# Layer 1 of a convolution and Mamba kernel: the norm's squares one step earlier, root and Newton behind the decay of scan 18, B's transposes behind a sum of y

## The chip, the core and the metric

The kernel runs on one core of a Trainium2 chip, as one launch. The metric is device time in microseconds (us), the median of several runs. A profile comes from one execution of its own, and its times are from the start of its span.

The engines of the core: PE (TensorE, matrix multiply; PEld is its weight load), DVE (VectorE), ACT (ScalarE, activation functions and copies), POOL (GpSimd) and SP (SyncE, which here only issues DMA transfers). Each engine runs its own queue of instructions in order and waits for others by semaphores. PE writes its results to PSUM, a small memory of eight banks; SBUF is the larger working memory.

## The reference

The input is 32 images of 96 channels and 56 x 56 pixels, in float32. Layer 0 is an inverted bottleneck convolution. Layer 1, in which the change lies, takes each image as a sequence of 3136 tokens with 96 channels and passes it through two Mamba blocks, then a fusion with a global branch and a batch norm. One block:

```
mu = seq.mean(-1); var = ((seq - mu) ** 2).mean(-1)
h = (seq - mu) * rsqrt(var + 1e-5) * ln_g + ln_b
xs, z = split(h @ in_w)                       # 192 channels each
xc = silu(causal_conv4(xs) + conv_b)
dt, Bm, Cm = split(xc @ xproj_w)              # 6, 16 and 16 columns
delta = softplus(dt @ dt_w + dt_b)
h_t = exp(delta * A) * h_(t-1) + delta * Bm * xc      # 192 channels x 16 states
y = (sum over states of h_t * Cm + Dp * xc) * silu(z)
seq = seq + y @ out_w
```

## The kernel before

**Units and steps.** In layer 1 each sequence is cut into four chunks of 784 tokens. A unit is one chunk in one of the two blocks, so there are 32 x 4 x 2 = 256 units, block 1 following block 0 at some distance. A unit holds 24 scans: three channel blocks k of 64 channels, in each four groups j of four states, and two halves p of the channels. Each scan is one instruction on DVE (line 1052) over 128 partitions (32 channels x 4 states) and 784 tokens, 1.84 us long.

**An order written out by hand.** The loop at the end of layer 1 goes through steps, one scan each. In a step it calls the work around that scan in a fixed sequence: inject (POOL: the product u x B for the two scans four steps on, line 1041), steps of the lists with small fractions, seed (ACT: D x xc into the PSUM bank of y, line 1086), decay (ACT: exp(delta x A) for the next scan, line 1004), bring (ACT: a copy cp of C into PSUM, line 1029), the bursts (Silu and Softplus with their table loads, lines 677 and 678), the scan, gated (DVE: y times the gate z, line 1110), product (DVE: state times C for the first 416 tokens, line 1060), save (ACT: last states, line 1077), rest (POOL: state times C for the other tokens, line 1068), fill (PE: the product u x B for the scans with j = 0, that is scans 0, 1, 8, 9, 16 and 17 of a unit, line 1018, into PSUM, tile bp), then listed steps with fractions from 0.05 to 0.08, reduce (PE: the sum over states into y, line 1099), and the listed steps with larger fractions. For scans with j = 0 the decay goes to SBUF (tile bx) and is computed two or three steps ahead. The PSUM tiles da and bp share two buffers, so each scan's decay or fill has to wait until the scan two before it is done.

**Listed steps.** prepare(n) returns the work that gets unit n ready as pairs (time, function). The time is counted in scans from the start of unit n - 2; the whole part names the step, the fraction the place in it. A time of -10.98 thus lies in step -11 with fraction 0.02. Modulo 24, the steps from -12 to -4 are scans 12 to 20 of an earlier unit, in which the work of the next units also runs. The steps that matter here:

- center(h), line 702: PE subtracts the channel mean from half h of the chunk (tile cen, PSUM).
- square(h), line 707: ACT squares it (tile sx, SBUF).
- variance, line 712: PE sums the squares with seven one-column matmuls, each of which is two instructions (tile var, PSUM). The fourth needs squares of both halves.
- root, lines 719 to 721: ACT adds epsilon (tile va), takes Ln and then Exp with scale -0.5, so that rs is about 1/sqrt(var). Line 723 copies the tail of the chunk before into xn.
- newton, lines 729, 731 and 734: three DVE operations refine rs.
- turn (line 744, PE, tile ct), normalise (line 751, ACT, tile sx_t), turn_back (line 757, PE, tile xn in PSUM), normal (line 761, ACT): the normalised chunk, channel by channel.
- project_bc (line 798, PE, tile bc) and store_bc (line 802, ACT, tile bcs, then two DMA stores): B, C and the input of delta, for the unit that follows.
- turn_b (line 822, PE, tile bt) and diagonal (lines 831 and 832, ACT): B's transposes for the diagonals of the fills; scatter sends them to DRAM eight steps later.
- project_dt (line 810), turn_u and keep_u (lines 848, 854 and 855): delta and the transposed u.

All of cen, var, ct, xn, xs, z, bc, bt, dt, ut and o share two PSUM banks (pool l1p). A new tile in this pool waits until the last reader of the tile that had the bank is done. Here bc takes over the bank of var.

In the step with scan 17, ACT's queue has, after the Silu burst of the step before: va, Ln, Exp, the tail copy, decay of scan 18, cp, a state copy, decay of scan 19, then bcs, four of normalise 0, decay of scan 20, cp, a state copy, the two copies of bt, three of normalise 1, and decay of scan 21.

Of the kernel before, what the change touches and what calls it, by code (L numbers as in the profile page):

```python
# [35 lines left out]
TK = 112  # L36
NK = LC // TK
# [23 lines left out]
def conv_mamba_kernel(ctx, tc, a, out):  # L61
# [43 lines left out]
    with ExitStack() as ph:  # L105
# [119 lines left out]
        for i in range(NHB):  # L225
            t = hp3.tile([128, H + 2, W + 2], F32, name=f"hpad{i}", tag=f"hpad{i}")
# [303 lines left out]
    with ExitStack() as ph:  # L530
# [14 lines left out]
        def bank(name):  # L545
            return pp.tile([128, 512], F32, name=name, tag="p")

        def wt(shape, tag, bufs, n):
            return work.tile(shape, F32, name=f"{tag}_{n}", tag=tag, bufs=bufs)
# [132 lines left out]
        def cols(h):  # L682
            return slice(h * HB, h * HB + HB)

        def prepare(n):
# [7 lines left out]
            d = data[n]  # L693
# [6 lines left out]
            def center(h):  # L700
                ps = d["cen", h] = bank(f"cen_{n}_{h}")
                pe.matmul(ps[:C, :HB], cen, seqs[c, i][:, cols(h)], start=True, stop=True)

            def square(h):
                if h == 0:
                    d["sq"] = wt([128, LC], "sx", 1, n)[:C]
                s.activation(d["sq"][:, cols(h)], d["cen", h][:C, :HB], AF.Square)
# [7 lines left out]
            def root():  # L715

                va = d["va"] = wt([TK, NK], "va", 1, n)
                rs = d["rs"] = d["var"][:TK, 16 : 16 + NK]
                s.activation(va, d["var"][:TK, :NK], AF.Identity, bias=epsc[:TK])
                s.activation(rs, va, AF.Ln)  # L720
                s.activation(rs, rs, AF.Exp, scale=-0.5)
                if q > 0:
                    s.copy(xn[:, : KC - 1], tails[i])

            def newton(step):
                va, rs = d["va"], d["rs"]
                if step == 0:
                    d["nw"] = wt([TK, NK], "nw", 1, n)
                    v.scalar_tensor_tensor(d["nw"], rs, -0.5, va, ALU.mult, ALU.mult)
                if step == 1:  # L730
                    v.tensor_mul(d["nw"], d["nw"], rs)
                if step == 2:
                    to = wt([TK, NK], "rs", 1, n)
                    v.scalar_tensor_tensor(to, d["nw"], 1.5, rs, ALU.add, ALU.mult)  # L734
                    d["rs"] = to
                    if q == 0:
                        g.memset(xn[:, : KC - 1], 0.0)
# [40 lines left out]
            def keep(tag, bufs, ps, k):  # L778
                if k == 0:
                    d[tag] = wt([128, NB, HB], tag, bufs, n)  # L780
                if tag == "dl":
                    s.activation(d[tag][:, k, :], d[ps, k][:, :HB], AF.Identity, bias=dp[:, i, k, 0:1])
                else:
                    s.copy(d[tag][:, k, :], d[ps, k][:, :HB])  # L784

            def gate(k):
                ps = d["zp", k] = bank(f"z_{n}_{k}")
                for h in range(2):
                    pe.matmul(  # L789
                        ps[h * 64 : h * 64 + 64, :HB], wz[:, i, k * 64 : k * 64 + 64],  # L790
                        xn[:, KC - 1 + h * HB : KC - 1 + h * HB + HB], start=True, stop=True,
                    )
# [73 lines left out]

            steps = [(-20.5, load)]
            for h in range(2):
                steps += [((-11.9, -10.94)[h], lambda h=h: center(h)), ((-10.98, -9.99)[h], lambda h=h: square(h))]
            steps += [(-9.94, variance), (-7.9, root), *[(t, lambda m=m: newton(m)) for m, t in enumerate((-6.3, -6.2, -6.1))]]  # L870
            for m in range(2):
                steps += [((-6.7, -5.5)[m], lambda m=m: turn(m)), (-5.7 + m, lambda m=m: normalise(m))]
                steps += [(-4.5 + m, lambda m=m: turn_back(m)), (-3.9 + m, lambda m=m: normal(m))]
# [4 lines left out]
            for k in range(NB):  # L878
                steps += [(t, lambda k=k, o=o: conv(k, o)) for o, t in taps[k]]
                steps += [((3.1, 5.1, 6.1)[k], lambda k=k: keep("xc", 3, "xs", k))]  # L880
                steps += [((11.06, 11.07, 12.06)[k], lambda k=k: gate(k)), ((12.01, 12.02, 13.01)[k], lambda k=k: keep("z", 3, "zp", k))]
            steps += [(17.6, project_bc), (18.2, store_bc), (18.6, turn_b), (19.2, diagonal)]
            for k in range(NB):
                steps += [((20.6, 21.5, 21.6)[k], lambda k=k: project_dt(k)), ((21.2, 22.1, 22.2)[k], lambda k=k: keep("dl", 1, "dtp", k))]
                steps += [((43.5, 53.6, 56.06)[k], lambda k=k: turn_u(k)), ((44.1, 54.2, 57.01)[k], lambda k=k: keep_u(k))]
# [59 lines left out]
        def place(t):  # L945
            k, r = divmod(t, 2 * SG)
            return k, r // 2, r % 2
# [38 lines left out]
        def by_pe(at):  # L986

            return place(at % NT)[1] == PEJ

        def lend(at):  # L990

            if by_pe(at) and at % 2 == 0:
                to = wt([128, 2, LC], "bx", 3, at)
                for p in range(2):
                    das[at + p] = to[:, p, :]

        def decay(at):

            n, t = divmod(at, NT)
            i, d = units[n][1], data[n]  # L1000
            k, j, p = place(t)
            if not by_pe(at):
                das[at] = dpool.tile([128, 2 * 512], F32, name=f"da_{at}", tag="da")[:, :LC]
            s.activation(das[at], d["delta", k][:, p, :], AF.Exp, scale=acol[:, j, i, 2 * k + p : 2 * k + p + 1])  # L1004
# [18 lines left out]
        def bring(at):  # L1023

            n, t = divmod(at, NT)
            k, j, p = place(t)
            if p == 1:
                cps[at] = cpool.tile([128, LP], F32, name=f"cp_{at}", tag="cp")
                s.copy(cps[at], data[n]["C", j][:, :LP])  # L1029
# [5 lines left out]
        def inject(at):  # L1035

            n, t = divmod(at, NT)
            k, j, p = place(t)
            if p == 0 and j != PEJ:
                bx = wt([128, 2, LC], "bx", 3, at)  # L1040
                g.tensor_mul(bx, data[n]["u", k], beside(data[n]["B", j]))  # L1041
                for p in range(2):
                    bxs[at + p] = bx[:, p, :]
# [35 lines left out]
        def seed(at):  # L1079

            n, t = divmod(at, NT)
            k, j, p = place(t)
            if j == 0 and p == 1:
                i, d = units[n][1], data[n]
                yps[k] = ypool.tile([128, 512], F32, name=f"y_{n}_{k}", tag="y")
                s.activation(yps[k][:, :HB], d["xc"][:, k, :], AF.Copy, scale=dp[:, i, k, 1:2])  # L1086
# [17 lines left out]
        def gated(at):  # L1104

            n, t = divmod(at, NT)
            k, j, p = place(t)
            if j == SG - 1 and p == 1:
                d = data[n]
                v.tensor_mul(d["z"][:, k, :], d["z"][:, k, :], yps.pop(k)[:, :HB])  # L1110

        total = len(units) * NT
        todo, early = {}, {}
        for n in range(len(units)):
            steps, bursts = prepare(n)
# [9 lines left out]
        def ahead(at):  # L1125

            return (2, 1) if at % NT == 0 else (3, 2)
# [5 lines left out]
        with tc.manual_schedule():  # L1133
            for at in range(min(todo), max(todo) + 1):
                for m in (2, 3):
                    if 0 <= at + m < total and by_pe(at + m) and (at + m) % 2 == 0 and ahead(at + m)[0] == m:
                        lend(at + m)
                if 0 <= at + 4 < total:
                    inject(at + 4)
                for u, step in todo.get(at, ()):  # L1140
                    if u < 0.05:
                        step()
                if 0 <= at - LAG < total:
                    seed(at - LAG)
                if 0 <= at + 1 < total and not by_pe(at + 1):
                    decay(at + 1)
                for x in range(at, at + 5):
                    pair = x // 2 * 2
                    if 0 <= x < total and by_pe(x) and pair - ahead(pair)[x - pair] == at:
                        decay(x)  # L1150
                if 0 <= at < total:
                    bring(at)
                for step in early.get(at, ()):
                    step()
                if 0 <= at < total:
                    scan(at)
                if 0 <= at - LAG - 1 < total:
                    gated(at - LAG - 1)
                if 0 <= at - 1 < total:
                    product(at - 1)  # L1160
                if 0 <= at - 2 < total:
                    save(at - 2)
                if 0 <= at < total:
                    rest(at)
                if 0 <= at + 1 < total and by_pe(at + 1):
                    fill(at + 1)
                for u, step in todo.get(at, ()):
                    if 0.05 <= u < 0.08:
                        step()
                if 0 <= at - LAG < total:  # L1170
                    reduce(at - LAG)
                for u, step in todo.get(at, ()):
                    if u >= 0.08:
                        step()
                for t, tag in BEFORE[at % NT]:
                    fetch(at + t, (tag,))
# [79 lines left out]
```

## Time and profile before

| what | value |
|---|---|
| median of three runs | 18147.85 us (18144.67 to 18149.34) |
| the profiled execution | 18136.26 us, span 18134.5 us |
| DVE, share of the span | 93% |
| POOL | 78% (14,115 of 14,950 us, 94%, from 2,900 to 17,850 us) |
| PE | 86% |
| ACT | 78% |
| first scan to last scan | 3023.2 to 17836.6 us |
| mean length of a unit | 57.87 us |

Layer 0 takes the first 2,900 us and isn't touched by the change. The profile lists groups of instructions by line, engine and tile, with their count, their busy time, the mean length of one in ns, the idle time of their engine just before them and what ended most of it. The list of waits sums idle time by who waited for whom: total us, number of times, longest. A timeline row gives the start, the length, the engine, the line, the operation with its tiles and shapes, and in brackets the idle time before it. A row of the windows gives the window, its length, each engine's busy time with its count of instructions (PE, PEld, DVE, ACT, POOL), the clock that TensorE was granted, the DMA engines' busy share and GB/s.

### The profile page before, as it was taken

How to read it: one execution, taken by the hardware profiler on the slowest of the kernel's cores; microseconds unless marked ns; L12 is line 12 of the kernel's file. 1: busy time of each engine (PE TensorE's matmuls, PEld its weight loads, DVE VectorE, ACT ScalarE, POOL GpSimd, SP SyncE). 2: the span in 40 equal slices, each digit the busy share in tenths (PEclk: the TensorE clock that was granted, in tenths of full speed). 3: DMA queues.
4: the chain of work that ended last, by engine and by line, in shares of the span. 5: the costliest groups of instructions: out<-in, count | busy, mean ns of one | idle time of the engine just before them, and what ended most of it. 6: DMA issues, size and time to landing. Idle time of an engine off the chain costs nothing.

```text
span 18134.5 us, 515855 instructions
## 1 busy us (share of the span) xinstructions
PE 15647.2 (86%) x212542; PEld 8205.4 (45%) x212542; DVE 16799.6 (93%) x12755; ACT 14155.9 (78%) x26476; POOL 14150.6 (78%) x6254
## 2 busy tenths in 40 slices
PE   9999998888888888888888888888888888888882
PEld 4444444444444444444444444444444444444441
DVE  9999996999999999999999999999999999999993
ACT  5555555888888888888888888888888888888884
POOL 0000003999999999999999999999999999999993
PEclk9999998999999999999999999999999999999995
DMA  1111113777777777777777777777777777777778
GB/s 35 29 29 29 29 29 93 186 184 187 182 185 182 184 187 184 183 184 183 184 186 184 183 183 182 185 187 184 184 183 183 184 186 184 183 183 183 185 184 219
DMA packets 1723535, 2893.15 MB, mean 160 GB/s; under 512 B 712886, under 2 KB 950670, under 8 KB 1714790
## 3 DMA queue, kind: packets, MB, share of 16 engines
q1 hardware_dynamic: 1712534, 2821.54, 60.4%
q0 software_dynamic: 6656, 38.54, 1.0%
q8 instruction: 1668, 27.33, 0.7%
q14 instruction: 693, 5.68, 0.1%
q10 hardware_dynamic: 1984, 0.07, 0.0%
HBM read 2402.42 MB, written 455.82 MB: 158 GB/s over the span
## 4 chain that ended last, share of the span: by engine, by line
PE 25%; ACT 19%; issue 11%; DMA 10%; DVE 8%; SPq 6%; POOL 4%; ACTq 0%; POOLq 0%; DVEq 0%
PE bp L1018 8%; DVE hh L1052 5%; ACT da L1004 5%; PE y L1099 4%; SPq L982 3%; ACT bx L1004 3%; DVE hc L1060 3%; PE bc L798 3%; PE z L789 3%; DMA deltab<-deltad 3%; PE o L909 2%; DMA bdiag<-bt 2%; SPq L969 2%; POOL hc L1068 2%; POOL bx L1041 2%
## 5 line engine op out<-in xcount | busy, mean ns | idle before, releaser
L1041 POOL TENSOR_TENSOR bx<-ub,B 128x1568 f32<-128x1568 f32 x2304 | 8172.1, 3547 | 16.3 <-DMA diag<-bdiag 13.2
L1052 DVE TENSOR_TENSOR_SCAN hh<-da,state,bx 128x784 f32<-128x784 f32 x3456 | 6273.7, 1838 | 144.8 <-ACT da L1004 133.3
L1068 POOL TENSOR_TENSOR hc<-hh,C 128x736 f32<-128x736 f32 x3072 | 5416.3, 1763 | 714.3 <-DVE hh L1052 398.1
L1004 ACT ACTIVATE da<-deltab,acol 128x784 f32<-128x784 f32 x4608 | 4249.3, 922 | 916.0 <-DVE hh L1052 914.0
L1018 PE MATMUL bp<-diag,ut 91*32 91x91 f32 (+1 forms) x98304 | 3005.8, 280 | 436.3 <-ACT ut L854 351.4
L1099 PE MATMUL y<-hc,rel 128*32 128x392 f32 x24576 | 2911.8, 546 | 522.1 <-ACT y L1086 517.8
L1018 PEld LDWEIGHTS bp<-diag,ut 91*32 91x32 f32 (+1 forms) x98304 | 2652.1, 123 | 1285.3 <-DVE hh L1052 524.1
L1060 DVE TENSOR_TENSOR hc<-hh,cp 128x832 f32<-128x832 f32 x3072 | 3071.8, 1000 | 0.1
L1052 DVE TENSOR_TENSOR_SCAN hh<-bx,state,bp 128x784 f32<-128x784 f32 x1152 | 2117.4, 1838 | 297.8 <-PE bp L1018 269.9
masks.py:197 POOL MEMSET eye<- 128x128 f32 x2 | 0.4, 205 | 2892.6 <-ACT x L427 2892.3
L773 PE MATMUL xs<-xn,wx 97*64 97x392 f32 x12288 | 2240.2, 507 | 0.4 <-ACT xc L784 0.4
L1052 DVE TENSOR_TENSOR_SCAN hh<-da,bx 128x784 f32<-128x784 f32 x1152 | 2025.2, 1778 | 70.6 <-ACT da L1004 65.5
L340 DVE SCALAR_TENSOR_TENSOR h<-hpad,hp,h 128x1568 f32<-128x1568 f32 x1024 | 1895.5, 1851 | 33.2
L1029 ACT COPY cp<-C 128x416 f32<-128x416 f32 x3072 | 1570.4, 511 | 10.3 <-DVE hc L1060 8.8
L1004 ACT ACTIVATE bx<-deltab,acol 128x784 f32<-128x784 f32 x1536 | 1463.4, 953 | 0.0
L773 PEld LDWEIGHTS xs<-xn,wx 97*64 97x64 f32 x12288 | 817.9, 137 | 1366.7 <-issue 1271.0
L1099 PEld LDWEIGHTS y<-hc,rel 128*32 128x32 f32 x24576 | 609.2, 115 | 1521.2 <-ACT y L1086 983.6
L307 PE MATMUL dw<-hpad,diag 32*32 32x392 f32 x36864 | 1111.3, 518 | 0.1
L798 PE MATMUL bc<-xc,wbc 64*64 64x392 f32 x3072 | 634.6, 547 | 318.8 <-DVE rs L734 295.0
L245 PE MATMUL c<-x,w 96*128 96x392 f32 x2048 | 774.2, 520 | 117.8 <-ACT hpad L252 95.8
L864 POOL TENSOR_TENSOR us<-dl,xc 128x392 f32<-128x392 f32 x768 | 788.2, 1026 | 90.4 <-ACT dl L677 90.4
L1052 DVE TENSOR_TENSOR_SCAN hh<-bx,bp 128x784 f32<-128x784 f32 x384 | 682.9, 1779 | 174.3 <-PE bp L1018 138.4
(195 smaller groups left out, 20108.1 us busy)
## 6 DMA issues: line engine op xcount, KB each, us to landing
ub<-ud SPq DMA_DIRECT2D x3072, 196.0 KB
deltab<-deltad SPq DMA_DIRECT2D x3072, 196.0 KB
C<-bcd SPq DMA_DIRECT2D x4096, 98.0 KB
diag<-bdiag SPq DMA_DIRECT2D x1024, 294.8 KB
B<-bcd SPq DMA_DIRECT2D x3072, 98.0 KB
deltad<-dl SPq DMA_DIRECT2D x512, 294.0 KB
ud<-us SPq DMA_DIRECT2D x1536, 98.0 KB
x<-in_x_dram SPq DMA_DIRECT2D x32, 1176.0 KB
```

The source lines that it names most:

```text
L307: pe.matmul(ps[r][to : to + 32, :HB], diag[src, n, t, :], hb[src, r0 : r0 + RB, dx : dx + W], start=t == 0, stop=t == 8, skip_group_check= ...
L340: v.scalar_tensor_tensor(acc, src, tap, acc, ALU.mult, ALU.add)
L773: pe.matmul(d["xs", k][h * 64 : h * 64 + 64, :HB], wx[:, i, o, k * 64 : k * 64 + 64], xn[:, o + h * HB : o + h * HB + HB], start=o == 0, s ...
L798: pe.matmul(ps[r, :HB], wbc[r, i, k], d["xc"][r, k, :], start=k == 0, stop=k == NB - 1)
L1004: s.activation(das[at], d["delta", k][:, p, :], AF.Exp, scale=acol[:, j, i, 2 * k + p : 2 * k + p + 1])
L1018: pe.matmul(ps[sg * DB : sg * DB + DB, o : o + z], d["ut", k][:z, b, h, p * DB : p * DB + DB], dg[:z, sg // 2, h, x : x + z, sg % 2], star ...
L1029: s.copy(cps[at], data[n]["C", j][:, :LP])
L1041: g.tensor_mul(bx, data[n]["u", k], beside(data[n]["B", j]))
L1052: v.tensor_tensor_scan(hhs[at - p][:, p, :], das.pop(at), bxs.pop(at), state[i][:, t : t + 1] if c % NQ else 0.0, ALU.mult, ALU.add,)
L1060: v.tensor_mul(hcs[at - 1][:, :, :LP], hhs[at - 1][:, :, :LP], beside(cps.pop(at)))
L1068: g.tensor_mul(hcs[at - 1][:, :, LP:], hhs[at - 1][:, :, LP:], beside(data[n]["C", j][:, LP:]))
L1099: pe.matmul(yps[k][r0 : r0 + DB, :HB], rel, hc[:, p, h * HB : h * HB + HB], start=False, stop=j == SG - 1, skip_group_check=True,)
```

## The change

Four things change in layer 1.

- square(1) moves from step -10 (scan 14) to step -11 (scan 13), right behind the decay of scan 14, and center(1) moves with it to a place ahead of it. The main loop gets a second place for listed steps, for fractions from 0.03 to 0.05, behind decay. Only these two steps fall into it.
- root moves from the end of the step of scan 16 to the end of the step of scan 17, so behind the decay of scan 18 and its cp. The three Newton operations move from the end of the step of scan 17 to the step of scan 18, behind scan 18 and the product of scans 16 and 17.
- the root's result rs is a tile "ra" of its own in SBUF; before, it was in the PSUM bank of var, from column 16 on.
- turn_b moves from the step of scan 18 to the step of scan 19, behind reduce. That reduce is the last sum of y for channel block 1, which the gate of that block needs. diagonal keeps its place.

On PE the order of center(1) stays as it was, and only bt changes places with four matmuls of y. On POOL the memset of xn's first columns, in units that begin a sequence, passes behind the next product u x B. SP's queue has the same order.

```
             def root():
                 va = d["va"] = wt([TK, NK], "va", 1, n)
-                rs = d["rs"] = d["var"][:TK, 16 : 16 + NK]
+                rs = d["rs"] = wt([TK, NK], "ra", 1, n)
...
             for h in range(2):
-                steps += [((-11.9, -10.94)[h], lambda h=h: center(h)), ((-10.98, -9.99)[h], lambda h=h: square(h))]
-            steps += [(-9.94, variance), (-7.9, root), *[(t, lambda m=m: newton(m)) for m, t in enumerate((-6.3, -6.2, -6.1))]]
+                steps += [((-11.9, -10.97)[h], lambda h=h: center(h)), ((-10.98, -10.96)[h], lambda h=h: square(h))]
+            steps += [(-9.94, variance), (-6.9, root), *[(t, lambda m=m: newton(m)) for m, t in enumerate((-5.95, -5.9, -5.85))]]
...
-            steps += [(17.6, project_bc), (18.2, store_bc), (18.6, turn_b), (19.2, diagonal)]
+            steps += [(17.6, project_bc), (18.2, store_bc), (19.15, turn_b), (19.2, diagonal)]
...
                 for u, step in todo.get(at, ()):
-                    if u < 0.05:
+                    if u < 0.03:
                         step()
                 if 0 <= at - LAG < total:
                     seed(at - LAG)
                 if 0 <= at + 1 < total and not by_pe(at + 1):
                     decay(at + 1)
+                for u, step in todo.get(at, ()):
+                    if 0.03 <= u < 0.05:
+                        step()
```

## The prediction

> **What bounds the kernel now.** I read the page's groups, then the waits, then the scans in order of time. A unit is one chunk of one layer: 24 scans, 256 units. VectorE is busy 14,091 of 14,950 us from 2,900 to 17,850 us, GpSimd 14,115; both set the pace.
>
> ```profile
> L1052 DVE TENSOR_TENSOR_SCAN hh<-da,state,bx 128x784 f32<-128x784 f32 x3456 | 6273.7, 1838 | 144.8 <-ACT da L1004 133.3
> L1068 POOL TENSOR_TENSOR hc<-hh,C 128x736 f32<-128x736 f32 x3072 | 5416.3, 1763 | 714.3 <-DVE hh L1052 398.1
> ```
>
> GpSimd's idle time ends mostly with a scan, so an earlier scan moves both engines until that 398.1 us (1.6 us a unit) is used up. What the scans and the stage around the change wait for:
>
> ```profile
> DVE hh L1052 <- PE bp L1018: 408.3, 535, 1.7
> PE bc L798 <- DVE rs L734: 295.0, 233, 2.7
> PE var L712 <- ACT sx L707: 266.7, 252, 1.1
> DVE hh L1052 <- ACT da L1004: 198.8, 487, 1.2
> ```
>
> Laid out 24 to a unit, the scans' idle means per unit are 0.46 us (scan 16), 0.27 (17), 0.18 (18), 0.36 (20), 0.13 (22), and 0.14 before the gate of channel block 1. Means hide three kinds of unit. The windows show why: TensorE's granted clock stands at 1.00 or 0.50.
>
> ```profile
> 10167.87:10174.70 6.83, 6.48 (x104) 5.51 (x108) 5.58 (x5) 6.78 (x8) 6.83 (x3) 0.50 0.97 276
> 9251.00:9260.00 9.00, 6.43 (x47) 3.75 (x49) 8.49 (x11) 8.20 (x23) 9.00 (x4) 1.00 0.93 255
> 10234.60:10244.90 10.30, 9.15 (x43) 5.41 (x44) 8.32 (x10) 7.31 (x21) 8.89 (x4) 0.58 0.83 224
> ```
>
> (The column before the last two is the clock.) Among 246 inner units, 84 are **kind F**: the clock halves at the fill (bp) of scan 16, which waits over 0.3 us (1.32 in the mean). 67 are **kind C**: it halves at the projection bc, whose matmuls take 3.2 us, not 2.2. 95 are **kind W**, neither. From scan 12 to the next unit's scan 0 they take 30.02, 30.60 and 28.67 us. The gate waits 71 times in all, about as often as kind C occurs.
>
> **The change, part by part.**
>
> *Square 1 a step earlier.* TensorE in a unit of kind F:
>
> ```profile
> 10166.49 0.75 PE L712 MATMUL var<-mean,sx 96*112 96x1 f32 x6
> 10168.22 1.65 PE L712 MATMUL var<-mean,sx 96*112 96x1 f32 x8 [0.98 <-ACT sx L707]
> 10169.80 2.85 PE L1018 MATMUL bp<-diag,ut 120*32 120x120 f32 x64
> ```
>
> Square 1 ran at 10167.69 behind two exponentials and a copy; now it follows the decay of scan 14 (ends 10166.47), its centre matmul long done. The variance goes on at about 10167.2, at full clock, and ends near 10168.2. The fill can't start then: its PSUM buffer frees when scan 14 ends, 10168.86. So it starts at 10168.9 instead of 10169.80. In ACT's queue behind the square stand the PE-scan exponential and copy cp of step 13, each 0.39 us later; cp is needed after scan 14, over 1 us on: hidden. Were it not, each unit would pay at most 0.39.
>
> *Root behind decay 18.* ACT's table load ends; then came va, Ln, Exp (0.26, 0.18, 0.15 us) and the tail copy, 0.7 us, then the decay. Now the decay comes first, and scan 18 starts 0.65 to 0.7 us earlier wherever scan 17 had ended. Newton's three operations (0.16 us each, 0.55 with gaps) pass from before scan 18 to behind product 17: the same VectorE time, so scan 19 gains only 0.2. What is late next is bc. Its PSUM bank was the variance's, and it waited for rs L734; now it waits for va, which stands behind decay (0.85 net), copy (0.45) and state copy: va ends 1.6 (W) and 1.75 us (C) after the table load, where rs had ended 1.3 and 1.4 after it. So bc is **0.2 later in W, 0.33 later in C**, 1.4 earlier in F. The root's writes in SBUF cost between a gain of 0.05 us and a loss of 0.1 on ACT: nearest rows, Ln into PSUM 179 ns, Exp 153, a copy 97x3 into SBUF 184. I take 0, by the copy; both ends are hidden by bc's start. Normalise now queues on ACT behind Newton (scan 18 + 3.2 us), and decay 20 behind normalise; the copy bcs ahead of it ends about then. GpSimd's memset of xn passes behind the next bx product (3.5 us), needed over 20 us later: hidden. SP's queue keeps its order.
>
> [...]
>
> *bt behind the sum of y.* A unit of kind C, TensorE and ACT:
>
> ```profile
> 10232.03 1.02 PE L744 MATMUL ct<-cen,seq 96*112 96x96 f32 x8
> 10235.17 3.24 PE L798 MATMUL bc<-xc,wbc 64*64 64x392 f32 x12 [2.12 <-DVE rs L734]
> 10238.99 1.43 PE L744 MATMUL ct<-cen,seq 96*112 96x96 f32 x6 [0.57 <-ACT bcs L802]
> 10240.21 1.38 PE L822 MATMUL bt<-bsel,bcs 128*120 128x8 f32 x8
> 10241.52 1.54 PE L1099 MATMUL y<-hc,rel 128*32 128x392 f32 x8
> ```
> ```profile
> 10238.83 1.04 ACT L751 ACTIVATE sx_t<-ct,rs 112x96 f32<-112x96 f32 x4
> 10239.74 0.95 ACT L1004 ACTIVATE da<-deltab,acol 128x784 f32<-128x784 f32 x1
> ...
> 10241.63 0.17 ACT L831 COPY bt<-bt 120x8 f32<-120x8 f32 x1 [0.40 <-PE bt L822]
> 10241.69 0.18 ACT L832 COPY bt<-bt 91x24 f32<-91x24 f32 x1
> 10241.76 0.80 ACT L751 ACTIVATE sx_t<-ct,rs 112x96 f32<-112x96 f32 x3
> 10242.45 0.93 ACT L1004 ACTIVATE da<-deltab,acol 128x784 f32<-128x784 f32 x1
> ```
>
> The gate no longer waits for y (0.55 us here). But ACT's copy of bt waits y's length longer: from 10241.63 to 10241.63 + 1.47 + 0.33 = 10243.43. Behind it stand normalise 1 and the decay of scan 21, which ends at 10245.2; scan 21 started at 10244.54, so it is **0.7 late** in place of the gate's 0.55 gain, and ut, xn, the seed of y and decay 22 follow 0.74 late. In kind W y takes 0.8 us, ACT idles 0.5 at bt, and decay 21 still ends 0.5 before scan 21: hidden, but for about 0.05 at scan 22. If W's cover went, it would pay up to 0.5.
>
> *The sum per kind, to the next scan 0.* C: bc + 0.33, bt, so + 0.74. W: scan 18 earlier is taken back at scan 20 by bc, + 0.05. F: scan 16 at 10171.85, not 10172.78; the fill of 17 is partly at half clock, so scan 17 gains 0.55; Newton ends at 10180.37 and normalise 0, decay 20 (1.04 and 0.95 with overlap) put scan 20 at 10182.38, not 10182.92: - 0.54. Mean: (67 x 0.74 + 95 x 0.05 - 84 x 0.54)/246 = + 0.04 us, x 256 = + 10 us.
>
> *Kinds that change.* The clock falls after TensorE has waited. Changes of clock lie on a grid of 3.41 us. Before bc, TensorE idles 2.12 us in this unit, 1.70 in one of kind W; both become about 0.3 longer, so about 0.33/3.41, a tenth of 246 units (24), pass to C, at 31.34 - 28.72 = 2.6 us each: + 63 us. From y to the fill the wait plus the one-column variance matmuls shrink by about 0.4: some 29 units pass from F to W, at 29.48 - 28.72 = 0.76 each: - 22 us. Together + 10 + 63 - 22 = + 51. Units shift against the grid, so the two shares are estimates; I round down to **+ 42 us**.
>
> [...]
>
> **Rivals.**
> 1. *Faster:* the variance's stall was what halved the clock at the fill. Without it kind F vanishes into W: - 1.30 in 84 units, with C's + 0.74 and W's + 0.05: - 0.22 a unit, - 57 us, 18,091. If C's bt finds slack as well, C loses only 0.33: - 0.33 a unit, - 85, 18,063. For: the 266.7 us wait goes. Against: the fill still waits for scan 14. It decides from the point where a third of F is gone without more of C.
> 2. *No change:* the kinds keep their shares: + 10, 18,158. For: a unit lasts 57.9 us, near 17 grid steps (58.0), so units may fall into step with the grid whatever is gained.
> 3. *Much slower:* half of W passes to C: 48 x 2.6 = 125 + 10: + 135, 18,283.
>
> **How the numbers follow.** The profiled execution took 18,136.26 us (span 18,134.5), 11.6 below the median of 18,147.85. Its differences are added to the median: forecast 18,147.85 + 42 = **18,190**. Chances: forecast 0.38, rival 1 0.27, rival 2 0.28, rival 3 0.07. A measurement of this kernel tells about 0.2% (36 us) from no change; so faster 0.27, same 0.28, slower 0.45. The range, with both signs: 18,060 to 18,285; the forecast's own case 18,184 to 18,230.
>
> **What would show it.** The wait of var for square 1 near 0; bc waiting for va, not rs; idle before scan 18 gone; ACT's copy of bt waiting several times its 0.11 us a unit; y's wait at the gate gone. Wrong if scan 22 comes no later in units with half clock at bc, or if scan 16 no longer waits at all.

## The result, and the profile after

The changed kernel takes **19,366.04 us** (19,352.38 to 19,377.94) against 18,146.26 (18,133.35 to 18,149.34) for the kernel before beside it: 6.7% slower, ratio 1.0673, 95% interval 1.0655 to 1.0692. That is 1,220 us more, far outside the predicted range. The profiled execution has a span of 19,350.6 us, 1,216 above that of before. A unit lasts 62.68 us in the mean, not 57.87.

First the page's groups of the kernel after (busy time, mean of one in ns, then the idle time before and its releaser):

```profile
L1068 POOL TENSOR_TENSOR hc<-hh,C 128x736 f32<-128x736 f32 x3072 | 5416.1, 1763 | 1939.9 <-DVE hh L1052 1237.8
L1052 DVE TENSOR_TENSOR_SCAN hh<-da,state,bx 128x784 f32<-128x784 f32 x3456 | 6269.0, 1837 | 103.3 <-ACT da L1004 91.2
...
L751 ACT ACTIVATE sx_t<-ct,rs 112x96 f32<-112x96 f32 x1792 | 471.3, 343 | 1059.0 <-DVE rs L734 1059.0
L729 DVE SCALAR_TENSOR_TENSOR nw<-ra,va 112x7 f32<-112x7 f32 x256 | 1133.7, 4428 | 79.1 <-ACT ra L721 79.1
...
L822 PE MATMUL bt<-bsel,bcs 128*91 128x8 f32 (+1 forms) x2048 | 365.7, 307 | 866.7 <-ACT sx_t L751 866.6
```

The scan and GpSimd's product take what they took. What is new is line 729, the first Newton operation: seven elements on 112 partitions, 4,428 ns in the mean. In the kernel before, among VectorE's groups, it was this:

```profile
L729 DVE SCALAR_TENSOR_TENSOR nw<-var,va 112x7 f32<-112x7 f32 x256 | 38.3, 150 | 93.3 <-ACT var L721 90.3
```

Line 729 grew by 1,133.7 - 38.3 = **1,095 us**. Nearly all the rest is idle time of VectorE, by the pages' busy times 19,350.6 - 17,909.0 = 1,441.6 us after and 18,134.5 - 16,799.6 = 1,334.9 before: 107 us, 0.42 us a unit. Together 1,202 of the 1,216. The stall does not look like a wait: the instruction has been issued and counts as busy, so VectorE's busy share stays at 93%, and no list of waits names it. Only the mean length tells.

The waits of the kernel after (us in total, times, longest) show who is late behind it:

```profile
POOL hc L1068 <- DVE hh L1052: 1237.8, 444, 3.8
...
ACT sx_t L751 <- DVE rs L734: 1059.0, 254, 5.8
...
PE bt L822 <- ACT sx_t L751: 866.6, 253, 5.2
DVE hh L1052 <- PE bp L1018: 642.7, 854, 13.1
...
PE bc L798 <- ACT va L719: 248.2, 183, 2.7
...
DVE hh L1052 <- ACT da L1004: 136.4, 485, 0.9
...
ACT bt L831 <- PE bt L822: 54.8, 203, 1.8
```

GpSimd now waits for a scan for 1,238 us (398 before), ACT's normalise for Newton for 1,059, and TensorE, whose bt stands behind the part of normalise that frees its bank, for 867. The wait of var for the square is no longer in the list, and bc waits for va, not for rs: both as predicted, and both small beside the rest.

One unit in time, VectorE first (start, length):

```profile
10018.04 1.00 DVE L1060 TENSOR_TENSOR hc<-hh,cp 128x832 f32<-128x832 f32 x1
10018.95 4.27 DVE L729 SCALAR_TENSOR_TENSOR nw<-ra,va 112x7 f32<-112x7 f32 x1
10023.25 0.17 DVE L731 TENSOR_TENSOR nw<-nw,ra 112x7 f32<-112x7 f32 x1
10023.45 0.17 DVE L734 SCALAR_TENSOR_TENSOR rs<-nw,ra 112x7 f32<-112x7 f32 x1
10023.53 1.84 DVE L1052 TENSOR_TENSOR_SCAN hh<-da,state,bx 128x784 f32<-128x784 f32 x1
```

and GpSimd in the same stretch:

```profile
10017.99 1.74 POOL L1068 TENSOR_TENSOR hc<-hh,C 128x736 f32<-128x736 f32 x1
10019.70 3.50 POOL L1041 TENSOR_TENSOR bx<-ub,B 128x1568 f32<-128x1568 f32 x1
10025.55 1.74 POOL L1068 TENSOR_TENSOR hc<-hh,C 128x736 f32<-128x736 f32 x1 [2.35 <-DVE hh L1052]
```

GpSimd's product bx ends at 10019.70 + 3.50 = 10023.20, line 729 at 10018.95 + 4.27 = 10023.22. Lines 731 and 734 have two SBUF inputs as well and take 0.17 us: GpSimd is then idle, since its next product needs scan 19, which stands behind Newton. So it goes in every unit: 253 of the 256 line-729 operations run beside GpSimd, each of them ends within 30 ns of the end of a GpSimd operation, and the other three (166 or 167 ns) run before the scans begin.

TensorE waits 3.40 us for normalise in this unit. After that it is at half clock, as the window shows (window, length, busy and count of PE, PEld, DVE, ACT and POOL, granted clock, DMA share, GB/s):

```profile
10024.74 1.49 PE L822 MATMUL bt<-bsel,bcs 128*120 128x8 f32 x8 [3.40 <-ACT sx_t L751]
...
10023.00:10031.00 8.00, 5.71 (x27) 3.73 (x31) 7.71 (x9) 7.12 (x21) 2.16 (x3) 0.50 0.62 166
```

So dt and the fill for the next scan 0 are late: that scan idles 1.13 us a unit (0.06 before). Part of this belongs to bt's new place: with it, but without the long line 729, scan 0 idles 0.39 us (e2b_cp_bank below). VectorE's other waits became about 0.6 us a unit shorter in sum.

### The profile page after: what moved, and what is told of

It reads as the page before. It is cut to its first block, busy times and chain, and to the rows that moved or that the text cites. A ratio compares the mean times of both kernels' runs of the same rounds, so it can differ in the third digit from the quotient of the medians.

```text
span 19350.6 us, 516104 instructions
## 1 busy us (share of the span) xinstructions
PE 16256.0 (84%) x212542; PEld 8494.7 (44%) x212542; DVE 17909.0 (93%) x12755; ACT 14250.3 (74%) x26476; POOL 14150.7 (73%) x6254
## 4 chain that ended last, share of the span: by engine, by line
PE 27%; ACT 18%; issue 14%; DVE 13%; DMA 6%; SPq 4%; POOL 3%; ACTq 0%; DVEq 0%; POOLq 0%
PE bp L1018 9%; PE y L1099 5%; ACT da L1004 4%; DVE hh L1052 4%; PE dt L810 4%; DVE hc L1060 4%; DVE nw L729 3%; POOL bx L1041 2%; ACT bx L1004 2%; ACT sx_t L751 2%; PE o L909 2%; SPq L969 2%; PE bt L822 2%; DMA bdiag<-bt 2%; PE z L789 2%
## 5 line engine op out<-in xcount | busy, mean ns | idle before, releaser
L1018 PE MATMUL bp<-diag,ut 91*32 91x91 f32 (+1 forms) x98304 | 3088.0, 284 | 655.1 <-ACT ut L854 401.1
L1099 PE MATMUL y<-hc,rel 128*32 128x392 f32 x24576 | 3080.3, 574 | 488.2 <-ACT y L1086 483.8
L1018 PEld LDWEIGHTS bp<-diag,ut 91*32 91x32 f32 (+1 forms) x98304 | 2764.0, 126 | 1500.8 <-DVE hh L1052 466.0
L773 PE MATMUL xs<-xn,wx 97*64 97x392 f32 x12288 | 2197.3, 499 | 0.6 <-ACT xc L784 0.4
L751 ACT ACTIVATE sx_t<-ct,rs 112x96 f32<-112x96 f32 x1792 | 471.3, 343 | 1059.0 <-DVE rs L734 1059.0
L729 DVE SCALAR_TENSOR_TENSOR nw<-ra,va 112x7 f32<-112x7 f32 x256 | 1133.7, 4428 | 79.1 <-ACT ra L721 79.1
L822 PE MATMUL bt<-bsel,bcs 128*91 128x8 f32 (+1 forms) x2048 | 365.7, 307 | 866.7 <-ACT sx_t L751 866.6
L810 PE MATMUL dt<-bcs,wd 64*64 64x392 f32 x3072 | 925.0, 723 | 0.7 <-ACT bt L832 0.6
```

Source lines behind the costliest of these rows:

```text
L773: pe.matmul(d["xs", k][h * 64 : h * 64 + 64, :HB], wx[:, i, o, k * 64 : k * 64 + 64], xn[:, o + h * HB : o + h * HB + HB], start=o == 0, s ...
L810: pe.matmul(ps[r, :HB], wd[r, i, k, :], d["bcs"][r, :], start=True, stop=True)
L1018: pe.matmul(ps[sg * DB : sg * DB + DB, o : o + z], d["ut", k][:z, b, h, p * DB : p * DB + DB], dg[:z, sg // 2, h, x : x + z, sg % 2], star ...
L1099: pe.matmul(yps[k][r0 : r0 + DB, :HB], rel, hc[:, p, h * HB : h * HB + HB], start=False, stop=j == SG - 1, skip_group_check=True,)
```

## The experiments

**Theory P**: line 729 now reads two inputs from SBUF, rs and va; before, rs was in PSUM. By P such an operation waits until GpSimd has ended what it reads from SBUF. **Rival T**: Newton's new place makes it long. Each ratio below is against runs of the kernel before taken beside it, whose medians lie between 18,149 and 18,158 us.

**e1_var_bank**, the changed kernel with rs back in var's bank:

```
-                rs = d["rs"] = wt([TK, NK], "ra", 1, n)
+                rs = d["rs"] = d["var"][:TK, 16 : 16 + NK]
```

> The changed kernel, with the root's result rs back in the PSUM bank of var. Theory P: the first Newton operation (line 729) is long because it reads two inputs from SBUF (va and rs) and then waits for GpSimd. With rs in PSUM it has one, and falls from a median of 4,308 ns to 140 to 170 ns. The bank is then held until Newton has ended, behind product 17, so bc waits for it: it starts about 3 us later than in the changed kernel (14.8 us after scan 12 there, 17.7 here), and a unit pays 1.5 to 3 us for that: 18,500 to 18,900 us. Rival T: the new place of Newton behind scan 18 and product 17 makes the operation long, whatever its operands: it stays above 4,000 ns, and the time is at or above 19,366 us.

Measured: 19,840.89 us, ratio 1.0929 (1.0915 to 1.0944). Instructions of line 729 in its trace (ns: shortest, median, longest):

```profile
L729 DVE SCALAR_TENSOR_TENSOR nw<-var,va x256: 153/157/166, 2962.8 to 19372.4; 112x7 f32<-112x7 f32 x128
```

Same place, rs in PSUM, and the operation is short: T falls. The time was missed by 940 us. bc waits 3.70 us a unit for Newton, as expected, but then runs at half clock in 255 of 256 units (3.4 us, not 2.2), and scan 20 idles 4.1 us behind bc, bcs, normalise and decay 20. Once Newton stands behind product 17, rs can't stay in var's bank.

**e2_spare_bank** and **e7_va_psum** were to put rs, or va, in spare columns of another PSUM bank. The index in their code named a step whose cp did not exist yet, so rs fell back to var's bank, and va to SBUF: e2_spare_bank is e1_var_bank over again (19,833.6 us, ratio 1.0925, 1.0910 to 1.0940), e7_va_psum the changed kernel (19,370.09, 1.0670, 1.0656 to 1.0685). So they add nothing on P and T.

> The changed kernel, with rs in spare columns (448 to 455) of the PSUM bank of the copy cp of step 17, so that neither var's bank nor SBUF holds it. All four edits of place stay. Theory P: line 729 takes 140 to 170 ns, bc still starts behind va, and the time is what the prediction's sum gave without the long operation, 18,100 to 18,250 us. Rival T: the place of Newton is what costs, line 729 stays above 4,000 ns and the time stays near 19,366 us.

> The changed kernel, with rs in SBUF as there, but va in spare PSUM columns of the bank of cp of step 17. Line 729 then reads one input from PSUM and one from SBUF, and line 731 still reads two from SBUF (nw and rs). Theory P: line 729 falls to 140 to 170 ns, and the wait for GpSimd moves whole to line 731, which goes from 0.17 to about 4.2 us; line 734 stays near 0.17; the time stays within 100 us of 19,366. Rival A: line 729 is long because it reads what ACT has just written to SBUF; then line 729 stays above 4,000 ns for rs, or, if va was what it waited for, both lines are short and the time falls to about 18,190.

**e2b_cp_bank**, with the right index (cp is the copy that product 17 reads; in a tile of 512 columns it leaves 96 spare):

```
+                at = (n - 3) * NT + 17
-                rs = d["rs"] = wt([TK, NK], "ra", 1, n)
+                rs = d["rs"] = spare[at][:TK, 448 : 448 + NK] if at in spare else d["var"][:TK, 16 : 16 + NK]
...
+                wide = spare[at] = cpool.tile([128, 512], F32, name=f"cp_{at}", tag="cp")
+                cps[at] = wide[:, :LP]
```

> The changed kernel with all its edits of place, but rs in spare columns (448 to 455) of the PSUM bank of the copy cp of step 17: neither in SBUF nor in var's bank. (The run labelled e2_spare_bank was to do this, but its index named a step not yet brought, and rs fell to var's bank as in e1_var_bank.) Theory P, two SBUF inputs: line 729 takes 150 to 170 ns, bc starts behind va, and the time is what the prediction's sum gave when Newton costs what it did, 18,190 us, between 18,100 and 18,285. Rival T, the changed order costs by itself as well: the time stays above 18,500 us though line 729 is short.

Measured: 18,399.2 us, ratio 1.0139 (1.0125 to 1.0154). The operation (line 730 here) in its trace:

```profile
L730 DVE SCALAR_TENSOR_TENSOR nw<-cp,va x253: 155/158/163, 3076.8 to 17879.4; 112x7 f32<-112x7 f32 x127
```

P holds for the operation: moving one 112x7 operand out of SBUF takes 19,366 - 18,399 = **967 us** off. The range for the time, 18,100 to 18,285, was missed: some 250 us are left that the prediction put at 42.

**e7b_va_cp_bank**, the changed kernel, rs in SBUF, but va in those spare columns:

```
-                va = d["va"] = wt([TK, NK], "va", 1, n)
+                va = d["va"] = spare[at][:TK, 448 : 448 + NK] if at in spare else wt([TK, NK], "va", 1, n)
```

> The changed kernel with rs in SBUF as there, but va in spare PSUM columns of the bank of cp of step 17 (the edit that did not take hold in e7_va_psum). Line 729 then reads one input from PSUM and one from SBUF; line 731 still reads two from SBUF (nw and rs). Theory P: line 729 takes 150 to 170 ns, and the wait moves whole to line 731, from 0.17 us to about 4.2 in the median, ending with a GpSimd operation each time; the time stays within 150 us of 19,366. Rival A, line 729 is long because it reads what ACT has just written to SBUF: line 729 stays above 4,000 ns, line 731 at 166.

Measured: 19,264.33 us, ratio 1.0616 (1.0600 to 1.0632). The first Newton operation, line 730, has a median of 154 ns (157 at most) in the 253 units where va lies in PSUM; the second stands on the page so:

```profile
L732 DVE TENSOR_TENSOR nw<-nw,ra 112x7 f32<-112x7 f32 x256 | 1054.1, 4118 | 8.9
```

The wait moved to the next operation with two SBUF inputs, a little shorter there (4,118 ns in the mean, not 4,428), and 253 of these again end within 30 ns of the end of a GpSimd operation. That ACT had just written rs does not matter: line 730 reads it at once.

**e8_memset**, the changed kernel with one GpSimd product as a memset. It leaves out u x B for the scans of channel block 2, group 3.

```
-                g.tensor_mul(bx, data[n]["u", k], beside(data[n]["B", j]))
+                if (k, j) == (2, 3):
+                    g.memset(bx, 0.0)
+                else:
+                    g.tensor_mul(bx, data[n]["u", k], beside(data[n]["B", j]))
```

> The changed kernel, rs in SBUF as there, but GpSimd's product u x B for the two scans of channel block 2, group j = 3 (the one that runs while line 729 waits) is a memset to zero instead: this part of the input to the states is left out. If line 729 waits for GpSimd operations that read SBUF and not for one that only writes it, it waits for the rest of product 17 alone: about 1 us in the median instead of 4.3, and the time falls by more than 800 us against 19,366, to 18,300 to 18,550. Rival, any GpSimd operation holds it: it ends with the memset, later than the rest of product 17 by the memset's whole length. [...]

Measured: 18,478.14 us, ratio 1.0179 (1.0166 to 1.0193), in the range of P. VectorE in one of its units:

```profile
10002.84 0.99 DVE L1063 TENSOR_TENSOR hc<-hh,cp 128x832 f32<-128x832 f32 x1
10003.75 0.77 DVE L729 SCALAR_TENSOR_TENSOR nw<-ra,va 112x7 f32<-112x7 f32 x1
10004.56 0.17 DVE L731 TENSOR_TENSOR nw<-nw,ra 112x7 f32<-112x7 f32 x1
```

and GpSimd:

```profile
10002.75 1.74 POOL L1071 TENSOR_TENSOR hc<-hh,C 128x736 f32<-128x736 f32 x1
10004.43 1.41 POOL L1042 MEMSET bx<- 128x1568 f32 x1
```

Line 729 ends at 10004.52, with the product (10004.49) and not with the memset (10005.84); line 731, two SBUF inputs, runs in 0.17 us beside the memset, and so it does in 253 of the 256 units (169 ns at most). This operation, which only writes, does not hold VectorE. The median of line 729 is 0.8 us.

**e3_sbuf_only**, the kernel before with that one line changed:

```
-                rs = d["rs"] = d["var"][:TK, 16 : 16 + NK]
+                rs = d["rs"] = wt([TK, NK], "ra", 1, n)
```

> The kernel before, with rs in SBUF as its only edit; root and Newton keep their places ahead of scan 18. Theory P: line 729 is issued 14.5 us after scan 12, while GpSimd's product bx runs from 13.0 to 16.5 in the mean; it waits for its end, about 2 us, 3.5 at most if a second GpSimd product is behind it more, and scan 18 is late by about as much: 1.5 to 2.5 us a unit, 18,500 to 18,800 us. Rival T: the place is what costs, line 729 stays at 150 to 170 ns and the time within 40 us of 18,146.

Measured: 19,644.22 us, ratio 1.0821 (1.0806 to 1.0836): alone worse than the whole change, and 844 us above the upper end of the expectation. Its page:

```profile
L729 DVE SCALAR_TENSOR_TENSOR nw<-ra,va 112x7 f32<-112x7 f32 x256 | 1499.8, 5858 | 85.4 <-ACT ra L721 83.2
```

I had it wait for the one operation in flight. Here is a unit, VectorE and GpSimd:

```profile
10033.70 6.71 DVE L729 SCALAR_TENSOR_TENSOR nw<-ra,va 112x7 f32<-112x7 f32 x1
10040.44 0.17 DVE L731 TENSOR_TENSOR nw<-nw,ra 112x7 f32<-112x7 f32 x1
```

```profile
10031.74 3.50 POOL L1041 TENSOR_TENSOR bx<-ub,B 128x1568 f32<-128x1568 f32 x1
10035.20 1.74 POOL L1068 TENSOR_TENSOR hc<-hh,C 128x736 f32<-128x736 f32 x1
10036.89 3.49 POOL L1041 TENSOR_TENSOR bx<-ub,B 128x1568 f32<-128x1568 f32 x1
10045.29 1.75 POOL L1068 TENSOR_TENSOR hc<-hh,C 128x736 f32<-128x736 f32 x1 [4.91 <-DVE hh L1052]
```

It waits through three GpSimd operations, of which two began after it, and comes free when GpSimd has nothing ready. In 208 of the 253 units beside GpSimd it goes through three or more; in the changed kernel 102 of 253 do, and 149 go through two. So the later place of the changed kernel is cheaper, 4,428 ns in the mean and not 5,858: fewer GpSimd operations are ready there. In the other 45 units line 729 is held for only 0.32 us in the mean, but then line 731 for 1.67 and line 734 for 3.42, through one GpSimd operation each.

**e4_square_only**, the kernel before with the square's part of the diff alone (with the new place in the main loop):

```
-                steps += [((-11.9, -10.94)[h], lambda h=h: center(h)), ((-10.98, -9.99)[h], lambda h=h: square(h))]
+                steps += [((-11.9, -10.97)[h], lambda h=h: center(h)), ((-10.98, -10.96)[h], lambda h=h: square(h))]
```

> The kernel before with the earlier square 1 (and center 1) as its only edit. By the prediction's steps the variance's wait for the square (266.7 us in all) goes and the fill of scan 16 starts 0.9 us earlier in a third of the units; scan 16's idle falls from 0.46 to under 0.25 us a unit, and the time by 20 to 60 us: 18,090 to 18,130. Rival, nothing gained since the scans behind it wait for the decays and bc: within 15 us of 18,150.

Measured: 18,088.7 us, ratio 0.9969 (0.9958 to 0.9981): **61 us faster** than 18,149.69 beside it, 1 us below the expected range. Scan 16 idles 0.17 us a unit in place of 0.46.

**e5_bt_only**, the kernel before with bt's place alone:

```
-            steps += [(17.6, project_bc), (18.2, store_bc), (18.6, turn_b), (19.2, diagonal)]
+            steps += [(17.6, project_bc), (18.2, store_bc), (19.15, turn_b), (19.2, diagonal)]
```

> The kernel before with B's transposes bt behind the sum of y as its only edit. By the prediction's step the gate's wait for y goes (0.14 us a unit), and the copy of bt on ACT waits for y's length more, so that decay 21 is 0.7 us late in units with half clock at bc, and by 0.05 in the others: + 50 us, 18,200. Rival, the gate's gain is kept: - 35 us, 18,115.

Measured: 18,374.35 us, ratio 1.0127 (1.0113 to 1.0141): **225 us slower**, where 50 was expected. Waits of this kernel:

```profile
DVE hh L1052 <- PE bp L1018: 577.6, 701, 13.7
...
ACT bt L831 <- PE bt L822: 172.7, 255, 2.2
```

and the second of them in the kernel before:

```profile
ACT bt L831 <- PE bt L822: 31.8, 72, 1.8
```

The copy's wait rose from 31.8 to 172.7 us in all, which is the size expected. But the scans' wait for fills rose as well, from 408.3 to 577.6, and scan 0 idles 0.49 us a unit, not 0.06. The means by kind tell where from (rows of the trace; us after scan 12, before and here). Kind C, 57 units: the copy of bt 21.05 and 22.76, scan 21 23.89 and 24.47, the fill for scan 0 28.52 and 30.49, scan 0 30.60 and 32.33. Kind W, 109 units: the copy 19.67 and 20.08, scan 21 22.51 and 22.53, but the first dt takes 1.52 us where it took 0.88; the fill starts at 27.37, not 26.16, scan 0 at 29.25, not 28.67. VectorE hardly sees the late copy; TensorE does, whose dt and fill for scan 0 are later by more than the copy is. How the late copy leads to the slow dt is not shown.

**e12_copies_late**, the kernel before with ACT's copies of bt behind normalise 1:

```
-            steps += [(17.6, project_bc), (18.2, store_bc), (18.6, turn_b), (19.2, diagonal)]
+            steps += [(17.6, project_bc), (18.2, store_bc), (18.6, turn_b), (19.35, diagonal)]
```

> The kernel before with one edit: ACT's two copies of bt (lines 831 and 832) stand behind the three of normalise 1 in ACT's queue, not ahead. bt keeps its place on TensorE, ahead of y. The transposes ut take over bt's PSUM bank, so they wait for these copies: about 0.5 us of idle on TensorE before ut, where there was none, while normalise 1 and decay 21 are no later on ACT. Theory C, the bt edit's 225 us come from TensorE's clock: idle before ut, beside that before the xn transposes and dt, makes the clock halve at dt; then the matmuls of dt (531 ns in the mean) rise above 590 ns, the fill of scan 0 is late by a microsecond in many units, and the time rises by 100 to 250 us: 18,250 to 18,400. Rival Q, they come from ACT's queue (normalise 1 and decay 21 behind the copies): then dt stays near 531 ns and the time within 40 us of 18,150.

Measured: 18,161.91 us, ratio 1.0008 (1.0000 to 1.0017); dt stays at 530 ns. The number is that of rival Q (ACT's queue), but the run does not decide against C (TensorE's clock): in kind W TensorE waits 0.38 us before ut, and the wait before the second half of xn falls from 0.78 to 0.45. The sum, 0.83, is nearly that of before (0.78); in e5_bt_only it is 1.11. A wait of 0.38 us at ut alone costs nothing that the time shows; whether some 0.3 us more of idle is what halves the clock at dt stays open. The sum alone can't be it: in kind F of e5_bt_only (80 units) the same two waits come to 1.11 us too, and dt stays at full clock in every unit.

**e10_root_only** (the kernel before with root and Newton moved and rs in cp's bank, as in e2b_cp_bank) and **e6b_bt_back** (e2b_cp_bank with bt at its old place, so root and square). The lines of the two:

```
-            steps += [(-9.94, variance), (-7.9, root), *[(t, lambda m=m: newton(m)) for m, t in enumerate((-6.3, -6.2, -6.1))]]
+            steps += [(-9.94, variance), (-6.9, root), *[(t, lambda m=m: newton(m)) for m, t in enumerate((-5.95, -5.9, -5.85))]]
...
-            steps += [(17.6, project_bc), (18.2, store_bc), (19.15, turn_b), (19.2, diagonal)]
+            steps += [(17.6, project_bc), (18.2, store_bc), (18.6, turn_b), (19.2, diagonal)]
```

> The kernel before with root behind the decay of scan 18 and Newton behind product 17, rs in the bank of cp; square and bt as before. If the parts add up (250 for all three, 225 for bt, - 61 for the square), the root's move costs 86 us: 18,236, between 18,190 and 18,280; decay 20 is late behind normalise, and scan 20 idles about 0.7 us a unit in place of 0.36. Rival, the prediction's step: scan 18 earlier in the third of units with half clock at the fill, so a gain of some 40 us: 18,110.

> The changed kernel with rs in the bank of cp (as in e2b_cp_bank) and with B's transposes bt back at their old place ahead of the sum of y: the square and the root are what is left of the change. If the parts add up, the 225 us that bt alone cost go from the 250 of e2b_cp_bank: 18,175 us, 18,140 to 18,210. Rival, bt costs only when bc is early or late: then bt behind y is no loss here and the time stays at 18,360 to 18,420. Line 730 at 150 to 170 ns in both.

Measured: 18,176.45 us, ratio 1.0011 (1.0002 to 1.0020), and 18,177.58 us, ratio 1.0011 (1.0002 to 1.0019). The second is where it was expected. The first is not: the root's move alone costs 18 us, not 86, nor does it gain 40. With the square it costs 20, so the square's 61 us are lost beside it: bc runs at half clock in 122 of the 246 inner units of e6b_bt_back, against 67 before and 79 in e10_root_only, and scan 20 idles 0.90 us a unit, not 0.36.

**e11_next_cp** and **e13_cp_behind** build on e4_square_only: rs goes into the bank of the next cp at root's old place, so that bc need not wait for Newton; the second also issues that cp behind Newton.

```
-                rs = d["rs"] = d["var"][:TK, 16 : 16 + NK]
+                at = (n - 3) * NT + 17
+                if at > 0:
+                    spare[at] = cpool.tile([128, 512], F32, name=f"cp_{at}", tag="cp")
+                rs = d["rs"] = spare[at][:TK, 448 : 448 + NK] if at > 0 else d["var"][:TK, 16 : 16 + NK]
...
-                if 0 <= at < total:
+                if 0 <= at < total and at % NT != 17:
                     bring(at)
...
                     if u >= 0.08:
                         step()
+                if 0 <= at < total and at % NT == 17:
+                    bring(at)
```

> The kernel before with the earlier square (as in e4_square_only) and, at root's and Newton's old places, rs in the bank of the next cp (that of step 17) instead of var's. bc then waits for va, not for Newton, with line 729 still at one SBUF input and 0.15 us. In e3_sbuf_only bc started 0.6 us earlier in this way. If the wait of bc is what halves the clock at bc in a third of the units, these fall below 40 of 246, scan 20's idle below 0.15 us a unit, and the time by 80 to 200 us against the 18,089 of e4_square_only: 17,890 to 18,010. Rival, other waits take the wait's place: within 25 us of 18,089.

> As e11_next_cp (earlier square; rs at root's old place in the bank of the next cp), but the copy cp of step 17 is issued behind Newton, so that Newton doesn't wait for a copy into its bank (0.86 us a unit in e11_next_cp, where line 732 waited for cp). Theory F, bc freed from Newton is a gain that this wait ate: scans 18 and 19 come up to 0.8 us earlier, bc stays at full clock in nearly all units, and the time falls by 50 to 200 us against the 18,095 of e11_next_cp: 17,900 to 18,045. Rival G, GpSimd or the fills set the pace: the time stays within 25 us of 18,095.

Measured: 18,094.76 us, ratio 0.9967 (0.9956 to 0.9979), and **18,042.65 us, ratio 0.9945 (0.9932 to 0.9959)**. In the first, a wait stands in the list where bc's was:

```profile
DVE nw L732 <- ACT cp L1033: 218.1, 188, 1.9
```

Newton waits there for the copy into the other columns of its tile, and the time is that of e4_square_only, as the run's rival had it. In the second this wait is gone. In both bc is at half clock in about 1 unit of 100, and scans 20 and 22 no longer idle. The second gains 107 us on the kernel before. Theory F (a gain of 50 to 200 us over e11_next_cp) is favoured at its small end but not shown: the medians differ by 52 us, the ratios by 0.0022, some 40 us, and their intervals just overlap. The fills of scans 16 and 17 now take back part (1.05 us of idle a unit, 0.73 before). This is the fastest version found.

## Why the prediction was wrong, point by point

| step | measured, against before |
|---|---|
| square and root together (e6b_bt_back) | + 20 us |
| bt behind y, on top (e2b_cp_bank less e6b_bt_back) | + 222 us |
| rs in SBUF, on top (after less e2b_cp_bank) | + 967 us |
| sum | + 1,209 of + 1,220 us |

- **The step that failed: that Newton's three operations take "the same VectorE time".** Of rs in SBUF I priced only the writes ("between a gain of 0.05 us and a loss of 0.1 on ACT"): who writes rs, and not who reads it. The writes' price held: Ln and Exp took 208 ns in the mean with rs in SBUF and 166 with rs in PSUM, 0.08 us a unit. The reads' price was put at nothing: Newton's row of 0.16 us was that of an operation with one input in PSUM, and with both in SBUF the first one took 4.4 us, which is 967 us of the time. The profile before had a hint: in layer 1 each scan, product, gate and Newton operation had at most one of its two input tensors in SBUF (da, bp, cp, y and rs were in PSUM), and GpSimd was busy beside them 94% of the time. No row there showed the price of a second one, so it needed a bound from GpSimd's rows (1.76 and 3.5 us), not none.
- **What holds such a read**: no row of before tells, the runs do. Line 732 of e7b_va_cp_bank, with two SBUF inputs, took 4.1 us in the mean beside GpSimd's products, which read SBUF, and in 253 units ended with one of GpSimd's operations; line 731 of e8_memset took 0.17 us beside the memset, which only writes. In the unit of e3_sbuf_only shown above one Newton operation was held for 6.71 us, through three GpSimd operations; in 45 other units of that run, three Newton operations were each held by one GpSimd operation alone.
- **bt behind y**: the mechanism was named (ACT's copy waits for y's length, decay 21 late by 0.7 in kind C), and its size at scan 21 was right (0.58). What failed is "ut, xn, the seed of y and decay 22 follow 0.74 late" and "+ 0.05" in W: by dt and the fill, which TensorE runs behind xn, scan 0 came 1.73 and 0.58 us later. 225 us, not some 50.
- **Square**: right. The wait went, scan 16 still waits for the scan two before it, and the gain of 61 us is near the 0.54 us of kind F (84 units, 47 us in all).
- **Root**: in e10_root_only scan 18 starts 0.67 us (kind C) and 0.59 us (W) earlier after scan 12 than before (0.65 to 0.7 forecast), and bc waits for va and starts 0.24 and 0.05 us later by the means of the kinds (0.33 and 0.2 forecast). The idle before scan 18 that was to go stays (0.16 us a unit, 0.18 before). Units pass to half clock at bc: 12 with the root alone, 55 with the square, 37 with bt too (e2b_cp_bank). The forecast for the whole change was 24; in the changed kernel itself there are 62 such units, 5 fewer than before. Units passing from W to C is the mechanism of rival 3, which I gave 0.07. Its 135 us are not reached in e6b_bt_back: the square's gain stands against it, and a unit of kind C is there 1.74 us longer than one of kind W, not 2.6.
- **The sum**: its terms gave + 51, and no row stands behind rounding it down to + 42. "Slower" had the largest chance, 0.45, but that it came out so is luck in the main: 967 of the 1,220 us come from the term that was put at nothing.
- **Rivals**: none had a new stall on VectorE. All four cases were about waits between engines that the profile already listed.

## What to carry to other kernels

When a small tile moves from PSUM to SBUF, look at every instruction that reads it: does it now have two SBUF inputs, and does GpSimd read SBUF beside it? Here line 729 then took 4,428 ns in the mean, where with one of its inputs in PSUM it took 150, and it ended with a GpSimd operation in 253 of 256 units; so price it at GpSimd's next instructions (1.76 and 3.5 us here), not at its own length. And an instruction that waited in this way counted as busy (VectorE 93% before and after): compare mean lengths of the same line before and after, not only waits.

## What the runs showed of the hardware

- VectorE's wait for GpSimd went through several GpSimd operations: 251 of 253 of line 729 in the changed kernel (4,428 ns in the mean) spanned two or more that followed each other without a gap, and GpSimd was idle for at least 2.29 us after each. In e3_sbuf_only 45 of 253 came free between two that followed each other without a gap, after 0.32 us in the mean, and the two Newton operations behind were then held by one GpSimd operation each (1.67 and 3.42 us). What decides which is open.
- The clock, by the clock records in the two traces. In the kernel before's, TensorE is granted 1.00 or 0.50, and each of the 935 changes comes a whole number of steps of 3.413 us after the one before it, to 1 ns. Between the first and the last scan it falls 424 times, and in the step ahead of each fall TensorE idles for 0.81 us or more (median 1.64); in the 3,216 steps at whose end it stays at 1.00, TensorE idles for 0.17 us in the median and for 1.83 at most. In the changed kernel's it falls 659 times, after 0.26 us or more (median 1.80). Falls follow idle time, but the two ranges overlap. At bc TensorE ran at half rate in 255 of 256 units of e1_var_bank, where bc waits 3.70 us a unit, and in about 1 unit of 100 of e13_cp_behind, where its wait for va is 12.9 us in all.
